# A conditioned transformer block on one core: in the QKV stages, token loads on GpSimd's queue, statistics three products sooner, one set of roots 17 products later

## The chip, the core and the metric

The kernel runs on one core of one Trainium2 chip. The metric is the time of one execution on the device in microseconds (us); of several runs the median is given. The core has a matrix engine (TensorE, in the views PE, with its weight loads as PEld), three more compute engines (VectorE, DVE; ScalarE, ACT; GpSimd, POOL), and SyncE (SP), which here only issues transfers. Each engine takes its instructions in order; transfers can be issued on the queue of SP or on that of GpSimd.

## The reference, cut to what matters

```python
mod = silu(condition) @ Wada + bada
sh_a, sc_a, gt_a, sh_m, sc_m, gt_m = split(mod, 6, axis=1)
xn = layernorm(x, g1, be1)
xm = xn * (1.0 + sc_a[:, None, :]) + sh_a[:, None, :]
x = x + gt_a[:, None, :] * attention(xm, Wqkv, Wproj, bproj)   # causal, 16 heads of 32
xn = layernorm(x, g2, be2)
xm = xn * (1.0 + sc_m[:, None, :]) + sh_m[:, None, :]
h = gelu(xm @ W1 + b1)
x = x + gt_m[:, None, :] * (h @ W2 + b2)
```

`x` has two rows of 2048 tokens with 512 features in float32, `condition` two rows of 512, and the MLP is 2048 wide inside.

## The kernel before, in words

**Stages.** The work runs in this order: QKV of row 0, attention of row 0, projection of row 0 (with the start of row 1's QKV mixed in), QKV of row 1, attention of row 1, projection of row 1, and the MLP over both rows. A row is 16 token tiles of 128 tokens, or four groups of 512 tokens (`NG`, `MTT` = 4 tiles to a group).

**A QKV group.** A group is six units: four of keys and queries, two of values. A unit is seven products of half size (`unit`, L1002), a scheme of Strassen's kind: seven products of sums of blocks in place of eight, into three PSUM banks a, b and c. `first` (L1059) copies a finished bank away on ScalarE, `last` (L1072, L1078) adds a later bank to that copy on VectorE, and `split` (L1064, L1066) makes a high and a low part, which are stored to HBM by SP (L1031). The seventh product of a unit is issued after the first two of the next unit (`run`, L1138). A unit has seven products, so a group has 42 (`STEPS`). The first unit of row 0 alone is done plainly, by eight products of 512 tokens (`plain`).

**What hangs on the products.** After each product `tick` (L1145) runs, with n counting the group's products, and issues what belongs there:

- n = 30: the tokens of the group after the next are loaded (`load_x`, L915), four transfers of 128 tokens on SP's queue. The four buffers named `x` are shared by all groups, so the loads wait until the group before has been transposed out of them.
- n = 10 to 13: the statistics of the next group, one tile each (`stats`, L951 and L216: `bn_stats`, then `bn_aggr` on VectorE); with the fourth, `inv_std` (L223) takes the root of the four variances on ScalarE, then reciprocal and shift on VectorE. For row 1, group 1 has its statistics made during the projection.
- n = 15 and 25: ScalarE scales the next group's first and last two tiles in place (`scaled`, L958, L964).
- n = 18 and 28: TensorE transposes them (`norm`, L970; `transpose`, L214), and the modulated tokens become operands (`xmT`).
- n = 36, 38, 40: sums of operand blocks for the next group (`token_sum`).
- then the stage's own `also`, and from the second group on the first scores of the attention (`score`), with their maxima on VectorE (L498, L504).

**Weight pieces.** `also` calls `pieces.tick` (L1277). `Pieces` (L1207) builds, beside the QKV stages, the sums of MLP weights that the MLP needs: a piece is loaded by SP (L1241), summed by GpSimd (`add`, L1246; L1253) and stored by GpSimd's queue (`store`, L1264; L1273). A tick takes one operation from the list, and two while more than 12 are left. Row 1's plan (L1580) loads and starts four pieces: room_2 at ticks 0 and 6, room_1 at 16 and 24, room_2 again at 47 and 56, room_3 at 74 and 80, ticks counted over all groups. In room_1 a piece is 17 operations: four additions, three times four more, and the store. Row 1's value weights (`load_wv`, L922 on; L936) also come by GpSimd's queue, and their sums (L949) are GpSimd's.

**Order.** Each engine's order is laid down when the program is built. A helper, `mm` for products and `act` for other instructions (L204, L208), pins an instruction behind what its engine was given just before. An instruction without it is placed by a scheduler, which may set it ahead of its place in the program when it holds it for ready. Products, the additions of pieces and the statistics made during projection are pinned; the loads of tokens and the statistics in `tick` are not.

**Projection.** `project_phase` (L1297) computes 16 tiles of one row, takes the statistics for the second norm into `mv2`, and calls `between` after each tile, which for row 0 starts row 1's first group. At its end `inv_std(mv2, ...)` (L1358) takes the roots of the row's 16 variances. The MLP is what uses them.

Of the kernel before, what the change touches and what calls it, by code (L numbers as in the profile page):

```python
# [27 lines left out]
def dit_block_kernel(  # L28
# [36 lines left out]
    nc = tc.nc  # L65
# [4 lines left out]
    NT = T // P  # L70
# [3 lines left out]
    MTT = MT // P  # L74
# [74 lines left out]
    mv2 = const.tile([P, B * NT, 2], F32, tag="mv2", name="mv2")  # L149
    rstd2 = const.tile([P, B * NT], F32, tag="rstd2", name="rstd2")  # L150
    shift1 = const.tile([P, B * NT], F32, tag="shift1", name="shift1")
    shift2 = const.tile([P, B * NT], F32, tag="shift2", name="shift2")
# [47 lines left out]
    def x_rows(n):  # L200
        t0 = (n % NT) * P
        return x[n // NT, t0 : t0 + P, :]
# [5 lines left out]
    def act(ins):  # L208

        return tc.keep_in_program_order(ins)  # L210
# [12 lines left out]
    def inv_std(mv, rstd, shift, lo, hi):  # L223
        nc.scalar.activation(rstd[:, lo:hi], mv[:, lo:hi, 1], AF.Sqrt, bias=eps)
        nc.vector.reciprocal(rstd[:, lo:hi], rstd[:, lo:hi])
        nc.vector.scalar_tensor_tensor(
            shift[:, lo:hi], mv[:, lo:hi, 0], -1.0, rstd[:, lo:hi], ALU.mult, ALU.mult
        )
# [669 lines left out]
    class Qkv:  # L898
# [13 lines left out]
                for n in (S1, S2, A22)  # L912
            }

        def load_x(self, g):  # L915
            xts = []
            for t in range(MTT):
                xt = self.qp.tile([P, D], F32, tag="x", name="x", bufs=4)
                nc.sync.dma_start(xt, x_rows(self.row.b * NT + g * MTT + t))
                xts.append(xt)  # L920
            self.xts[g] = xts

# [190 lines left out]
        def values(self, g, t):  # L1113
# [22 lines left out]
            return self.unit(product, first, last, first)  # L1136

        def run(self, hp, also, early=()):  # L1138

            row = self.row  # L1140
            late = []
            for g in range(NG):
                at = [0]

                def tick():  # L1145
                    n, at[0] = at[0], at[0] + 1
                    if n >= self.STEPS:
                        return
                    if n == 30 and g + 2 < NG:
                        self.load_x(g + 2)  # L1150
                    if g + 1 < NG:
                        if n == 3 and g + 1 not in self.xts:
                            self.load_x(g + 1)
                        if 10 <= n < 10 + MTT and g + 1 > row.b:
                            self.stats(g + 1, n - 10)
                        if n in (15, 25):
                            self.scaled(g + 1, n // 25)
                        if n in (18, 28):
                            self.norm(g + 1, n // 28)()
                        sums = {36: S1, 38: S2, 40: S3}  # L1160
                        if n in sums:
                            self.token_sum(g + 1, sums[n])
                    elif n == 28:

                        row.rows(0)
                        act(nc.scalar.activation(first, eps, AF.Exp))
                    if g > 0 and n == 2:
                        self.token_sum(g, A22)
                    if n > 9 and self.loads:
                        self.loads.pop(0)()  # L1170
                    also(g, n)
                    if g > 0 and n >= 7:


                        past, of = n - 6, self.STEPS - 7
                        if g == 1:
                            row.score(row.count(cum[0] * past / of, 0))
                        else:
                            past += of * (g - 2)
                            row.score(  # L1180
                                row.count(
                                    cum[0] + (cum[2] - cum[0]) * past / (2 * of),
                                    1 if g == 2 and n < 25 else 2,
                                )
                            )

                for u in range(C + 2):
                    if (g, u) in early:
                        for k, step in enumerate(self.plain(g, u, hp)):
                            step()  # L1190
                            if k:
                                tick()
                        self.token_sum(g, S3)
                        continue
                    if u < C:
                        steps = self.keys_and_queries(g, u, hp)
                    else:
                        steps = self.values(g, u - C)
                    for step in steps[:2] + late + steps[2:6]:
                        step()  # L1200
                        tick()
                    late = steps[6:]
            for step in late:
                step()
            assert not self.loads
# [91 lines left out]
    def project_phase(row, psum, between):  # L1297

        b = row.b
        with pool(f"proj{b}") as pp:
            n = 0
            ats = list(row.at_s)
            rbs = {1: row.rb_s[1], 2: row.old_queries(), 3: row.rb_s[0]}
            rows_x = [b * NT + i * TQ + t for i in last_order for t in range(TQ)]
            xts = list(row.xt_s)

            def tokens(upto):  # L1310
                while len(xts) < min(upto, NT):
                    xt = pp.tile([P, D], F32, tag="xt", name="xt", bufs=6)
                    nc.sync.dma_start(xt, x_rows(rows_x[len(xts)]))
                    xts.append(xt)

            row.load_sums(len(units) - 1, len(units))
            tokens(TQ + 6)
            for k, i in enumerate(last_order):
                if k in (0, 1):

                    at = pp.tile([P, C, QB], F32, tag="at", name="at", bufs=2)
                    nc.sync.dma_start(at, od[b][last_order[k + 2]])
                    ats.append(at)
                at = ats[k]
                for t in range(TQ):

                    if n == 0:
                        nc.sync.dma_start(rbs[2], wide_d[b][last_order[2]])
                        nc.sync.dma_start(
                            rbs[3][:, : C - 1], wide_d[b][last_order[3]][:, : C - 1]  # L1330
                        )
                    elif n == 3:
                        row.invert(len(units) - 1, len(units))
                    elif n == 4:
                        row.widen(len(units) - 1, rbs[3][:, C - 1, :])

                    tokens(n + 6)
                    nt, xt = rows_x[n], xts[n]
                    if k > 0:
                        act(nc.gpsimd.tensor_tensor(xt, xt, bgate, ALU.add))  # L1340
                    ps = psum.tile([P, D], F32, tag="mm", name="ps_o")
                    for c in range(C):
                        mm(
                            ps, at[:, c, t * P : (t + 1) * P], row.wproj[:, c, :],
                            start=(c == 0), stop=(c == C - 1),
                        )
                    nc.vector.tensor_tensor(xt, ps, xt, ALU.add)
                    stats(pp, xt, nt, mv2, True)
                    nc.sync.dma_start(x1d[nt], xt)
                    if k + 1 < NQ:  # L1350
                        d = ats[k + 1][:, t, :]
                        act(
                            nc.gpsimd.tensor_tensor(d, d, rbs[k + 1][:, t, :], ALU.mult)
                        )
                    between(n)
                    n += 1
        lo, hi = b * NT, (b + 1) * NT
        inv_std(mv2, rstd2, shift2, lo, hi)  # L1358


    row = Row(0)
    with pool("wada") as wp, pool("qkv0") as qp, pool("hl0") as hp, pool(
# [113 lines left out]
        def also(g, n):  # L1476

            if (g, n) == (0, 7):
                for k in range(4):
                    qkv.weight_sum(nc.gpsimd, k, slice(0, P))  # L1480
            pieces.tick()
            if g == 0 and n == 22:
                load_wada(2, 5)
            elif g in (1, 2) and n == 10:
                qkv.columns = modulation(g + 1)
            elif g in (1, 2) and n == 14:
                qkv.columns()
                if g == 1:
                    load_wada(3, 4)
                else:  # L1490
                    scale_shift(a2, c2, r_g2, r_be2, 3, 4)
# [36 lines left out]
    past, row = row, Row(1)  # L1528
    with pool("qkv1") as qp, pool("ps_qkv1", bufs=6, space=PSUM) as ps_mm:
# [24 lines left out]
        def also(g, n):  # L1554
            if (g, n) == (0, 10):
                qkv.value_weight_sums()
            pieces.tick()

        with pool("hl1") as hp:
# [769 lines left out]
```

## Time and profile before

| quantity | value |
|---|---|
| median of 3 runs | 2249.56 us (2248.82 to 2253.02) |
| the profiled execution | 2252.46 us |
| its span in the trace | 2250.7 us |
| granted TensorE clock, mean | 0.999 |
| instructions | 33467 |
| VectorE busy | 1537.3 us, 68% |
| ScalarE busy | 1003.6 us, 45% |
| GpSimd busy | 1298.3 us, 58% |

The span runs from the first to the last instruction of the one execution that was profiled. A row of a timeline has start and length in us from the span's start, the engine, the line of the kernel, the operation, its tiles (out<-in) with partitions and elements, the count (`x4` is four in a row), and in brackets the idle time of the engine ahead of it with what ended that. `SPq` and `POOLq` are the queues' own work of issuing. Busy times are of the whole span; a share of 68% says nothing of which wait sets the end in one stage.

### The profile page before, as it was taken

How to read it: one execution, taken by the hardware profiler on the slowest of the kernel's cores; microseconds unless marked ns; L12 is line 12 of the kernel's file. 1: busy time of each engine (PE TensorE's matmuls, PEld its weight loads, DVE VectorE, ACT ScalarE, POOL GpSimd, SP SyncE). 2: the span in 40 equal slices, each digit the busy share in tenths (PEclk: the TensorE clock that was granted, in tenths of full speed). 3: DMA queues.
4: the chain of work that ended last, by engine and by line, in shares of the span. 5: the costliest groups of instructions: out<-in, count | busy, mean ns of one | idle time of the engine just before them, and what ended most of it. 6: DMA issues, size and time to landing. Idle time of an engine off the chain costs nothing.

```text
span 2250.7 us, 33467 instructions
## 1 busy us (share of the span) xinstructions
PE 2210.1 (98%) x12057; PEld 1429.4 (64%) x12057; DVE 1537.3 (68%) x3309; ACT 1003.6 (45%) x2012; POOL 1298.3 (58%) x807
## 2 busy tenths in 40 slices
PE   7999999999999999999999999999999999999998
PEld 5887555555543588855555555345787787688687
DVE  4678766777757667777677767663685585576576
ACT  4434555555564253365665556614322422331410
POOL 4253998998983696299989898444105204304210
PEclk9999999999999999999999999999999999999999
DMA  8787142231324799532324113363353354353433
GB/s 274 247 277 193 44 92 70 62 85 48 107 96 135 247 308 321 152 83 67 80 67 104 48 46 131 108 233 127 114 174 131 125 182 147 106 187 126 159 126 109
DMA packets 160510, 311.57 MB, mean 138 GB/s; under 512 B 16544, under 2 KB 48844, under 8 KB 158552
## 3 DMA queue, kind: packets, MB, share of 16 engines
q1 hardware_dynamic: 155488, 285.53, 41.8%
q0 software_dynamic: 4480, 23.36, 2.7%
q8 instruction: 95, 1.56, 0.3%
q14 instruction: 71, 0.58, 0.1%
q10 hardware_dynamic: 376, 0.55, 0.1%
HBM read 229.95 MB, written 87.29 MB: 141 GB/s over the span
## 4 chain that ended last, share of the span: by engine, by line
PE 88%; DVE 4%; POOL 3%; DMA 2%; ACT 1%; issue 1%; SPq 0%; DVEq 0%; ACTq 0%; POOLq 0%
PE ps_a L206 26%; PE st L206 18%; PE ps_b L206 12%; PE o L206 10%; PE s L206 9%; PE ps_c L206 4%; PE sm L206 3%; PE ps_o L206 3%; DVE junk L498 1%; POOL ee L695 1%; PE ps_xt L214 1%; ACT e L670 1%; DVE mx L504 1%; PE ps_o L214 1%; DVE stat L218 1%
## 5 line engine op out<-in xcount | busy, mean ns | idle before, releaser
L670 ACT ACTIVATE e<-st 128x512 f32<-128x512 f32 (+1 forms) x1152 | 575.1, 579 | 362.6 <-PE st L206 319.2
L504 DVE TENSOR_REDUCE mx<-s 128x1 f32<-128x512 f32 x576 | 381.6, 686 | 193.4 <-PE s L206 192.4
L695 POOL TENSOR_TENSOR ee<-ee,e 128x2048 f32<-128x2048 f32 x106 | 485.8, 4583 | 10.4 <-ACT e L670 4.4
L206 PE MATMUL st<-qst,kst 128*128 128x512 f32 (+3 forms) x1280 | 408.8, 386 | 0.0
L206 PE MATMUL s<-kst,qst 128*128 128x512 f32 (+3 forms) x1046 | 380.5, 395 | 6.1 <-DVE mx L504 3.7
L206 PE MATMUL ps_a<-sum,w 128*128 128x256 f32 (+1 forms) x1088 | 328.7, 431 | 0.1
L206 PE MATMUL o<-e,vv 128*32 128x512 f32 (+3 forms) x2560 | 293.2, 537 | 0.3 <-POOL e L682 0.3
L206 PEld LDWEIGHTS st<-qst,kst 128*128 128x128 f32 x1280 | 228.5, 188 | 97.7 <-issue 66.0
L498 DVE CUSTOM_DVE_ANT_0 junk<-s,causal 128x128 bf16<-128x128 f32 (+3 forms) x470 | 220.7, 470 | 61.0 <-PE s L206 47.0
L1797 POOL TENSOR_TENSOR sum<-w 128x256 f32<-128x256 f32 x30 | 22.1, 738 | 395.2 <-PE ps_a L206 263.8
L206 PEld LDWEIGHTS s<-kst,qst 128*128 128x128 f32 x1046 | 194.9, 188 | 71.1 <-DVE mx L504 17.0
L206 PEld LDWEIGHTS ps_a<-sum,w 128*128 128x128 f32 x1088 | 204.5, 190 | 40.1 <-issue 11.4
L695 POOL TENSOR_TENSOR ee<-e 128x2048 f32<-128x2048 f32 x42 | 192.5, 4583 | 43.2 <-ACT e L670 42.3
L206 PEld LDWEIGHTS <-sel 32*128 32x128 bf16 x1152 | 29.5, 91 | 197.0 <-issue 196.1
L2016 ACT ACTIVATE h<-h,cols 128x512 f32<-128x512 f32 x120 | 76.8, 711 | 136.0 <-DVE h L1718 136.0
L504 DVE TENSOR_REDUCE mx<-st 128x1 f32<-128x512 f32 x192 | 131.0, 683 | 0.6
L682 POOL TENSOR_SCALAR_AFFINE_SELECT e<-e 128x512 f32<-128x512 f32 x128 | 83.3, 669 | 67.6 <-ACT e L670 67.5
L206 PE MATMUL st<-fold,sel 32*128 32x512 bf16 (+1 forms) x1152 | 117.5, 372 | 1.3
L206 PEld LDWEIGHTS o<-e,vv 128*32 128x32 f32 x2560 | 59.1, 108 | 92.4 <-issue 73.0
L1718 DVE TENSOR_TENSOR h<-c,ps_b 128x256 f32<-128x256 f32 x90 | 37.9, 421 | 103.5 <-PE ps_b L206 103.0
L1066 POOL TENSOR_TENSOR lo<-lo,hi 128x512 fp32r<-128x512 f32 x32 | 40.6, 1274 | 103.9 <-ACT hi L1064 102.0
L206 PE MATMUL ps_b<-sum,w 128*128 128x256 f32 (+1 forms) x384 | 95.0, 383 | 0.0
(237 smaller groups left out, 3590.2 us busy)
## 6 DMA issues: line engine op xcount, KB each, us to landing
qst<-q SPq DMA_DIRECT2D x128, 256.0 KB
kst<-k SPq DMA_DIRECT2D x128, 256.0 KB
w<-w1d SPq DMA_DIRECT2D x32, 896.0 KB
w<-w2d SPq DMA_DIRECT2D x28, 1024.0 KB
w<-w2d SPq DMA_DIRECT2D x28, 768.0 KB
q<-hi SPq DMA_DIRECT2D x32, 256.0 KB
q<-lo SPq DMA_DIRECT2D x32, 256.0 KB
k<-hi SPq DMA_DIRECT2D x32, 256.0 KB
```

The lines of the kernel that those rows point to most:

```text
L206: return tc.keep_in_program_order(nc.tensor.matmul(*args, **kw))
L214: return tc.keep_in_program_order(nc.tensor.transpose(dst, src, ident[:n, :n]))
L218: ins = nc.vector.bn_stats(st, xt)
L498: nc.vector.tensor_tensor_reduce(junk[:, :w], x, causal[:, QB - w :], 1.0, MASKED, ALU.add, ALU.max, m,)
L504: self.vector(nc.vector.tensor_reduce(m, x, axis=AX.X, op=ALU.max))
L670: act(nc.scalar.activation(e4[:, h, :w], sts[h][:, :w], AF.Exp))
L682: nc.gpsimd.affine_select(d, d, pattern=[[0, HC], [1, P]], compare_op=ALU.is_ge, fill=0.0, base=0, channel_multiplier=-1,)
L695: act(nc.gpsimd.tensor_tensor(dst, x, y, ALU.add))
L1066: engine.tensor_tensor(lo, d, hi.bitcast(F32), ALU.subtract)
L1718: act(nc.vector.tensor_tensor(dst, x, y, ALU.add))
L1797: act(engine.tensor_tensor(dst, u, v, op))
L2016: nc.scalar.activation(d[j], d[j], AF.Gelu, bias=col(r_b1 + half * HF + fs[j], 1))
```

## The change

Three things are edited. The loads at n = 30 are issued on GpSimd's queue instead of SP's, in both rows. The statistics begin at n = 7 instead of 10 in all groups but the first, and the first scaling moves from 15 to 12 with them; where the row's number equals the group's (row 0's first group, row 1's second), the statistics are pinned. And the roots of row 0's projection variances are taken at n = 16 of row 1's first group, not at the end of row 0's projection; row 1's stay where they were.

```diff
-        def load_x(self, g):
+        def load_x(self, g, queue=nc.sync):
             xts = []
             for t in range(MTT):
                 xt = self.qp.tile([P, D], F32, tag="x", name="x", bufs=4)
-                nc.sync.dma_start(xt, x_rows(self.row.b * NT + g * MTT + t))
+                queue.dma_start(xt, x_rows(self.row.b * NT + g * MTT + t))
                 xts.append(xt)
             self.xts[g] = xts
...
                     if n == 30 and g + 2 < NG:
-                        self.load_x(g + 2)
+                        self.load_x(g + 2, nc.gpsimd)
                     if g + 1 < NG:
                         if n == 3 and g + 1 not in self.xts:
                             self.load_x(g + 1)
-                        if 10 <= n < 10 + MTT and g + 1 > row.b:
-                            self.stats(g + 1, n - 10)
-                        if n in (15, 25):
+                        s0 = 7 if g else 10
+                        if s0 <= n < s0 + MTT and g + 1 > row.b:
+                            self.stats(g + 1, n - s0, row.b == g)
+                        if n in (s0 + 5, 25):
                             self.scaled(g + 1, n // 25)
...
                     between(n)
                     n += 1
-        lo, hi = b * NT, (b + 1) * NT
-        inv_std(mv2, rstd2, shift2, lo, hi)
+        if b:
+            inv_std(mv2, rstd2, shift2, NT, 2 * NT)
...
         def also(g, n):
             if (g, n) == (0, 10):
                 qkv.value_weight_sums()
+            elif (g, n) == (0, 16):
+                inv_std(mv2, rstd2, shift2, 0, NT)
             pieces.tick()
```

## The prediction

> **What bounds the kernel now.** I read the page's first part to see which engine has slack, then PE's timeline through the two QKV stages, where the edits lie, then the queues that feed them.
>
> ```profile
> span 2250.7 us, 33467 instructions
> PE 2210.1 (98%) x12057; PEld 1429.4 (64%) x12057; DVE 1537.3 (68%) x3309; ACT 1003.6 (45%) x2012; POOL 1298.3 (58%) x807
> ```
>
> TensorE is busy in 98% of the span: an edit that issues no fewer products can win only the idle time that it closes, 40.6 us in all, and only the part that lies in the QKV stages. PE's timeline of row 0's QKV stage has these stops (time, duration, line, tiles, and in brackets the idle time ahead and who ended it):
>
> ```profile
> 18.28 8.83 PE L206 MATMUL ps_qk<-xmT,wqk 128*128 128x512 f32 x16 [1.78 <-DVE xmT L269]
> ...
> 80.42 0.33 PE L214 MATMUL ps_xt<-ident,x 128*128 128x128 f32 x1 [1.01 <-ACT x L964]
> 81.13 0.98 PE L214 MATMUL ps_xt<-ident,x 128*128 128x128 f32 x7 [0.38 <-ACT x L964]
> ...
> 117.26 1.92 PE L206 MATMUL ps_mod<-vv,sc 128*32 128x512 f32 x16 [0.95 <-DVE mx L504]
> ```
>
> The transposes at 80.42 wait for tokens scaled by ScalarE (1.01 + 0.38 = 1.39). The 0.95 ahead of 117.26 is put down to a maximum on VectorE, which itself stood behind a statistic; its row comes below. Row 1's stage:
>
> ```profile
> 772.07 1.03 PE L206 MATMUL ps_b<-t,wqk 128*128 128x256 f32 x4
> 775.46 1.13 PE L206 MATMUL ps_a<-t,wqk 128*128 128x256 f32 x4 [2.36 <-ACT lo L1059]
> ...
> 825.55 1.89 PE L206 MATMUL ps_a<-t,wqk 128*128 128x256 f32 x8
> ...
> 829.15 0.33 PE L214 MATMUL ps_xt<-ident,x 128*128 128x128 f32 x1 [0.56 <-ACT x L964]
> 829.86 0.98 PE L214 MATMUL ps_xt<-ident,x 128*128 128x128 f32 x7 [0.38 <-ACT x L964]
> ...
> 868.61 0.50 PE L206 MATMUL s<-kst,qst 128*128 128x512 f32 x1 [0.72 <-DVE mx L504]
> ```
>
> Stops of 2.36, 0.94 and 0.72. All that the change can win is therefore 2.36 + 1.39 + 0.95 + 0.94 + 0.72 = 6.36 us, 0.28% of the span.
>
> **The change part by part.**
>
> *The projection's roots.* The longest stop has its cause on ScalarE:
>
> ```profile
> 774.83 0.31 ACT L224 ACTIVATE rstd<-mv,eps 128x16 f32<-128x16 f32 x1 [7.74 <-DVE mv L221]
> ```
>
> The root of row 0's 16 variances waited for the last projection statistic, and the copies of PE's first products (L1059), by which PE's banks come free, stood behind it. The move issues the same three instructions (root, reciprocal, shift) 17 products later, at 16 of row 1's first group, where the variances have long been there; ScalarE is then busy 31.54 of 67.00 us (window below), so 0.31 goes beside PE. Who needs the roots is the MLP, over a thousand us later. Gain 2.36 at most, 0 if the root, which nothing pins, is set back to where it was.
>
> *Row 0's loads.* These are SP's issues of the tokens of groups 2 and 3:
>
> ```profile
> 61.36 1.82 SPq L919 DMA_DIRECT2D x<-in_x_dram  x4
> ...
> 109.96 4.42 SPq L919 DMA_DIRECT2D x<-in_x_dram  x4
> ```
>
> They stood behind stores of keys and queries. The window view shows POOL free here and full in row 1 (length; busy us of PE, PEld, DVE, ACT and POOL with counts; clock, DMA share, GB/s):
>
> ```profile
> 783.00:850.00 67.00, 66.06 (x326) 58.05 (x324) 42.40 (x87) 31.54 (x73) 66.28 (x82) 1.00 0.96 309
> 62.60:100.00 37.40, 36.01 (x184) 29.86 (x183) 20.72 (x62) 17.19 (x39) 0.59 (x1) 1.00 0.85 252
> 850.00:861.00 11.00, 11.00 (x53) 9.61 (x53) 6.79 (x21) 3.81 (x9) 0.20 (x2) 1.00 0.89 355
> ```
>
> POOL does 0.59 us in 37.40, so row 0's loads leave as soon as the old tokens are transposed, and I let the stops of 1.39 and 0.95 go: −2.3. Against that: group 1's statistics, due at 10, are now pinned there. Before, the first ran at
>
> ```profile
> 22.78 0.68 DVE L218 BATCH_NORM_STATS2 stat<-x 128x6 f32<-128x512 f32 x1
> ```
>
> while PE was still in the 16 plain products of 18.28, that is, well ahead of its place in the program. Pinned, the four come later; I take +0.3, one ScalarE root in the way (0.31), between 0 and 1.39 (the stop of 80.42, as the nearest of its kind). Row 0: **−2.0**, and from −2.3 up to +3.1 where a statistic that nothing pins runs ahead of its tokens by the three products it gained (3 × 1.03, row 772.07).
>
> *Row 1, group 2.* Its tokens now leave from SP, and their statistics run here:
>
> ```profile
> 816.59 1.83 SPq L919 DMA_DIRECT2D x<-in_x_dram  x4
> ...
> 860.62 1.82 SPq L919 DMA_DIRECT2D x<-in_x_dram  x4
> ```
>
> ```profile
> 819.49 0.69 DVE L218 BATCH_NORM_STATS2 stat<-x 128x6 f32<-128x512 f32 x1
> ...
> 824.20 0.40 DVE L1078 TENSOR_TENSOR lo<-lo,ps_a 128x256 f32<-128x256 f32 x1
> ```
>
> From SP's issue to the first statistic pass 2.90 us. On POOL the loads take their turn behind additions of MLP weight pieces. The plan starts room_1's 17 operations at tick 24; two a tick at 24, 25 and 26, one at 27, 28 and 29: nine additions come ahead of tick 30, and the tenth is pinned behind the loads. In POOL's timeline:
>
> ```profile
> 780.21 2.90 POOL L936 DMA_DIRECT2D wv<-in_L_cond_Wqkv_dram  x4 [7.09 <-DMA kst<-in_L_cond_W_dram]
> ...
> 812.60 10.79 POOL L1253 TENSOR_TENSOR vv<-vv 128x512 f32<-128x512 f32 x9
> 823.34 0.56 POOL L1273 DMA_DIRECT2D w2d<-vv  x1
> ```
>
> Two of room_1's additions lie just ahead of the nine at 812.60; these take 10.79 / 9 = 1.20 each, so the ninth of the room ends at 812.60 + 7 × 1.20 = 821.0. Four issues take 2.90 (row 780.21); the last begins at about 821.0 + 3 × 0.73 = 823.2. That POOL is busy 66.28 of 67.00 says that it gives no earlier turn unless the loads are set between additions. Landing, for the same 256 KB and for larger stores, takes (last number, us):
>
> ```profile
> wv<-in_L_cond_Wqkv_dram POOLq DMA_DIRECT2D x4, 256.0 KB, 7.6
> ```
>
> ```profile
> w2d<-vv POOLq DMA_DIRECT2D x4, 448.0 KB, 3.6
> ```
>
> The first is of this stage and size, the second of 883 to 893 us. I take 7.6, the nearest: the last token tile is there at about 830.8, between 826.8 and 830.8; as the queue is in use, not all four need the whole 7.6, and I put it at 830. The statistics are now pinned, three products sooner: VectorE stands at them from about 816 until the tokens come, and with it everything behind: maxima of the scores, the joins of L1072 and L1078, by which PE gets banks. The last statistic (0.69) and some six short operations of 0.40 (row 824.20) follow, 3.1 us, an estimate; PE, whose product of 825.55 needs them, goes on at 833.1 to 833.5: +7.6 to +8.0. The stop of 0.94 at 829 falls into it: **+7.0**, between +3.4 (landing 3.6) and +7.0. It takes in the 2.36 won on the roots, as the tokens come at POOL's time and not at PE's.
>
> [...]
>
> [...] The lines view of 783 to 850 has this for GpSimd's issues:
>
> ```profile
> L1273 POOL DMA_DIRECT2D w2d<-vv x6 | 3.3, 548 | 0.0
> ```
>
> [...]
>
> *Row 1, group 3.* The loads go behind room_2's last additions instead of SP's 860.62, from about 851 on (POOL does 0.20 us between 850 and 861; with the first loads it gets there up to 2.9 later). They may end the 0.72, or cost: three products (3.1) plus the slower landing (7.6 − 2.90 = 4.7), +7.8, if these unpinned statistics are set ahead of their tokens. The nearest row for a statistic that waits for tokens:
>
> ```profile
> 115.92 0.69 DVE L218 BATCH_NORM_STATS2 stat<-x 128x6 f32<-128x512 f32 x1 [1.57 <-DMA x<-in_x_dram]
> ```
>
> I take **+1.5**. SP is freed of four issues of 0.46 in each of four groups, 7.3 us of a queue whose waiting is not on PE's path: 0.
>
> *Sum.* −2.0 + 7.0 + 1.5 = +6.5: 2252.46 + 6.5 = 2258.96 for the profiled execution, and on the median, 2249.56 (2.90 lower), **2256.0**.
>
> **The rivals.**
>
> *A, faster: the loads are early.* If the scheduler sets row 1's loads between the additions as soon as the old tokens are transposed, they land before 820 and every stop goes: −6.4, **2243.2**. For it: only additions and products are pinned, not loads. Against it: an addition that is ready and first in the program goes first, and POOL always has one. It decides if the last load starts before some 815: 815 + 7.6 + 3.1 is 825.7, when PE gets there now. If then the root also stays where it was, the change does not do what it says there, −4.0 and 2245.6, still inside A.
>
> *B, no change: the loads are late but quick.* With 3.6 for landing the tokens are there at 826.8, PE goes on at 829.9, +3.4; the third group wins its 0.72: −2.0 + 3.4 − 0.7 = +0.7, **2250.3**. For it the row of 883 to 893, against it the row of the same size, 7.6, at a DMA share of 0.96. [...]
>
> *C, slower still.* The third group's statistics run ahead of their tokens: −2.0 + 7.0 + 7.8 = +12.8, **2262.4**. For it: nothing pins them, and 22.78 shows such ones well ahead of their place. Against it: POOL is free from 850 on.
>
> **How the numbers follow.** Forecast 0.36 (its own range 2253.6, with −2.3 + 7.0 − 0.7, to 2261.2, with row 0 at +3.1), A 0.20, B 0.27, C 0.17. A measurement of this kernel can tell about 0.2%, 4.5 us, from no change, so faster lies under 2245.1 and slower over 2254.1. A gives 0.19 faster and 0.01 same; B 0.27 same; the forecast 0.35 slower and 0.01 same; C 0.17 slower: 0.19, 0.29, 0.52. The range runs from 2244.0 (it leaves out half of A, 0.10) to 2264.0 (half of C, where row 0 is at +3.1 too, 0.08).
>
> **What would show it.** Roots: no root of 16 columns near 774, no stop of 2.36, and one such root some 15 us later. Row 0: issues of tokens on POOL right behind the transposes, and no stop at 80 or ahead of 117. Group 2 of row 1: four issues on POOL between 821 and 824 behind nine additions of room_1, a statistic whose releaser is the DMA of x near 830, and behind it a PE stop of 5 to 8 us released by VectorE. If the issues come before 815, A holds; if the landing is near 3.6, B. If the DMA's landing is 7.6 and PE still does not stop, the chain through the pinned statistics is wrong.

## The result, and the profile after

Over five runs each the changed kernel took a median of 2280.58 us (2274.27 to 2286.7) against 2250.58 (2248.82 to 2253.33): a ratio of 1.0134 with a 95% interval of 1.0113 to 1.0156, slower by 30 us. The forecast had the sign and a fifth of the size. The profiled execution of the changed kernel took 2286.7 us, the longest of its five, so sums made in its trace come to 34 us, not 30.

TensorE's work is the same (12057 products), so the time must be in its stops and its clock (granted 0.993 in the mean, 0.999 before). The first lines of the page after:

```profile
span 2285.0 us, 33456 instructions
## 1 busy us (share of the span) xinstructions
PE 2221.7 (97%) x12057; PEld 1435.7 (63%) x12057; DVE 1539.9 (67%) x3309; ACT 1003.6 (44%) x2012; POOL 1303.2 (57%) x823
```

PE is busy 11.6 us longer with the same products, and the span has grown by 34.3. Where that happens is read off a fixed point of each group, the start of its transposes (L214) in PE's timelines of both kernels (groups are numbered from 0, as in the code; some expectations below call row 1's group 2 its second group):

| transposes | before | after | after − before |
|---|---|---|---|
| row 0, group 1, first | 38.92 | 41.34 | +2.42 |
| row 0, group 1, second | 48.43 | 53.18 | +4.75 |
| row 0, group 2, first | 80.42 | 88.27 | +7.85 |
| row 0, group 3, first | 129.35 | 140.05 | +10.70 |
| row 1, group 0 (within the projection), second | 746.30 | 758.06 | +11.76 |
| row 1, group 1, first | 790.24 | 800.31 | +10.07 |
| row 1, group 2, second | 839.83 | 854.87 | +15.04 |
| row 1, group 3, first | 873.58 | 903.94 | +30.36 |
| projection of row 1 (transposes there) | 1480.10 | 1513.67 | +33.57 |

What lies between these stages, and the MLP, adds about 1 us and less each. Row 0 loses 8.3 us between the first and the fourth line, row 1 gains 1.7 where the roots stood, then loses 5.0 in group 2, 15.3 in group 3 and 3.2 behind it; 2.4 lie ahead of all this (last section). The stops of PE that carry these steps, in PE's timeline after:

```profile
41.34 0.33 PE L214 MATMUL ps_xt<-ident,x 128*128 128x128 f32 x1 [1.58 <-ACT x L964]
42.04 1.41 PE L214 MATMUL ps_xt<-ident,x 128*128 128x128 f32 x7 [0.38 <-ACT x L964]
...
62.66 3.55 PE L206 MATMUL ps_a<-wv,t 128*128 128x256 f32 x8 [2.40 <-DVE vv L1134]
```

```profile
785.52 1.13 PE L206 MATMUL ps_a<-t,wqk 128*128 128x256 f32 x4 [0.67 <-ACT lo L1059]
...
831.52 2.00 PE L206 MATMUL ps_a<-t,wqk 128*128 128x256 f32 x8 [1.43 <-DVE lo L1078]
839.91 2.00 PE L206 MATMUL ps_a<-t,wqk 128*128 128x256 f32 x8 [1.60 <-DVE lo L1078]
...
869.98 2.07 PE L206 MATMUL ps_b<-wv,t 128*128 128x256 f32 x4 [13.84 <-DVE lo L1072]
...
926.33 0.61 PE L206 MATMUL s<-kst,qst 128*128 128x512 f32 x1 [3.17 <-DMA qst<-q]
```

The stop of 2.36 is down to 0.67. In its place stands one of 13.84, put down to a join of VectorE (L1072). VectorE's own timeline shows what the join stood behind:

```profile
851.08 0.08 DVE L498 DVE_READ_ACCUMULATOR2_ANT mx<- 128x1 f32 x1
866.70 0.69 DVE L218 BATCH_NORM_STATS2 stat<-x 128x6 f32<-128x512 f32 x1 [15.54 <-DMA x<-in_x_dram]
...
869.51 0.42 DVE L1072 SCALAR_TENSOR_TENSOR lo<-ps_b,lo 128x256 f32<-128x256 f32 x1
```

For 15.54 us VectorE did nothing but wait for the tokens of row 1's last group, with the join that PE needed behind two of the statistics and their maxima. Row 0 shows the same on a smaller scale:

```profile
48.98 0.69 DVE L218 BATCH_NORM_STATS2 stat<-x 128x6 f32<-128x512 f32 x1 [3.36 <-DMA x<-in_x_dram]
...
60.32 0.69 DVE L218 BATCH_NORM_STATS2 stat<-x 128x6 f32<-128x512 f32 x1 [8.07 <-DMA x<-in_x_dram]
```

There the loads themselves leave sooner than before: GpSimd issues those of group 2 at 43.82 and 54.65, two each, right behind the transposes, where SP's stood at 61.36.

A group's statistics are due at n = 7 of the group ahead of it, yet these stand at a place of VectorE's order that PE reaches in the middle of the group before that one. How far ahead is counted in the instruction order of the built programs: the joins of VectorE (L1072, L1078 and L1134, three to a unit) ahead of the four statistics of a group, counted from the start of row 0:

| statistics of | before | changed | e2, queue alone | e4, all pinned |
|---|---|---|---|---|
| row 0, group 2 | 19 to 21 | 6 to 12 | 6 to 12 | 18 |
| row 0, group 3 | 36 | 24 to 27 | 24 to 27 | 36 |
| row 1, group 2 | 90 to 93 | 90 | 81 to 84 | 90 |
| row 1, group 3 | 109 to 111 | 96 to 101 | 96 to 101 | 108 |

Nine to thirteen joins are three to four units, 21 to 30 products, not the three products that the diff names. The one group of these that the change pins (row 1, group 2) is not ahead.

### The profile page after: what moved, and what is told of

It is laid out like the page before. It is cut to its first block, busy times and chain, and to the rows that moved or that the text cites. A ratio compares the mean times of both kernels' runs of the same rounds, so it can differ in the third digit from the quotient of the medians.

```text
span 2285.0 us, 33456 instructions
## 1 busy us (share of the span) xinstructions
PE 2221.7 (97%) x12057; PEld 1435.7 (63%) x12057; DVE 1539.9 (67%) x3309; ACT 1003.6 (44%) x2012; POOL 1303.2 (57%) x823
## 4 chain that ended last, share of the span: by engine, by line
PE 85%; DVE 4%; POOL 4%; DMA 3%; issue 2%; ACT 1%; SPq 1%; DVEq 0%; POOLq 0%; ACTq 0%
PE ps_a L206 24%; PE st L206 18%; PE ps_b L206 11%; PE o L206 10%; PE s L206 9%; PE ps_o L206 4%; PE sm L206 3%; PE ps_c L206 3%; POOL ee L695 1%; DVE junk L498 1%; PE ps_xt L214 1%; ACT e L670 1%; DMA x<-in_x_dram 1%; DVE mx L504 1%; PE ps_o L214 1%
## 5 line engine op out<-in xcount | busy, mean ns | idle before, releaser
L1066 POOL TENSOR_TENSOR lo<-lo,hi 128x512 fp32r<-128x512 f32 x32 | 40.6, 1272 | 125.7 <-ACT hi L1064 122.5
```

The source lines that it names most:

```text
L1066: engine.tensor_tensor(lo, d, hi.bitcast(F32), ALU.subtract)
```

## The experiments

**Theory P (placement).** With the loads on GpSimd's queue the scheduler holds the tokens for ready soon after their buffers are free, and sets the unpinned statistics there; VectorE then waits for loads that are late, and what follows in its order waits behind them (15.54 us above). **Rival W**: the loads themselves are too late on GpSimd's queue, wherever the statistics stand. **Rival S**: taking the statistics three products sooner is the cost.

**e1, the roots alone.**

```diff
-        inv_std(mv2, rstd2, shift2, lo, hi)
+        if b:
+            inv_std(mv2, rstd2, shift2, NT, 2 * NT)
...
+            elif (g, n) == (0, 16):
+                inv_std(mv2, rstd2, shift2, 0, NT)
```

> Only the roots of row 0's projection variances move; the loads stay on SP, the statistics at 10. Theory P (placement: with the loads on GpSimd's queue the unpinned statistics are set some 12 joins, four units, ahead of their place and hold VectorE until the tokens land): 1 to 2.4 us faster than before, the stop of 2.36 gone, all else as before. Rival W (the loads themselves come too late on GpSimd's queue): the same. Rival S (the statistics three products sooner are what costs): the same. It prices the move alone.

Measured: 2251.72 against 2252.06, ratio 0.9999 (0.9991 to 1.0008). The stop is down from 2.36 to 0.67 as with the change, but the root has not moved: in e1 it stands at 771.40, still directly ahead of the copies of L1059. What P expected, 1 to 2.4 us, is not seen (0.3 by the medians), and what the move is worth this run cannot tell. No theory is hurt; the edit is not what costs.

**e2, the queue alone.**

```diff
-                        self.load_x(g + 2)
+                        self.load_x(g + 2, nc.gpsimd)
```

> Only the queue of the loads changes; statistics at 10 and unpinned, roots as before. P: all three groups' statistics of row 1 and row 0 that have such loads are set ahead (row 1's group 2 too, which the change had pinned), so at least as slow as the change: 25 to 45 us over before. W: 15 to 30 us over before. S: within 5 us of before.

Measured: 2292.75, ratio 1.0186 (1.0172 to 1.02), 41 us slower, and 11 more than the whole change, each against its own runs of before. That lies in P's range and above W's; S falls, as nothing is sooner here. VectorE waits in row 1's group 2 too, which the change had pinned:

```profile
825.33 0.69 DVE L218 BATCH_NORM_STATS2 stat<-x 128x6 f32<-128x512 f32 x1 [18.48 <-DMA x<-in_x_dram]
...
874.74 0.69 DVE L218 BATCH_NORM_STATS2 stat<-x 128x6 f32<-128x512 f32 x1 [10.82 <-DMA x<-in_x_dram]
```

**e3, the statistics sooner alone** (with the scaling at 12 and the two pins, loads on SP).

```diff
-                        if 10 <= n < 10 + MTT and g + 1 > row.b:
-                            self.stats(g + 1, n - 10)
-                        if n in (15, 25):
+                        s0 = 7 if g else 10
+                        if s0 <= n < s0 + MTT and g + 1 > row.b:
+                            self.stats(g + 1, n - s0, row.b == g)
+                        if n in (s0 + 5, 25):
```

> Only the statistics move to 7 (with the first scaling at 12 and the two pins); loads on SP, roots as before. P and W: within 4 us of before, stops of the kind of 1 us only. S: 20 us or more over before.

Measured: 2253.92 against 2252.06, ratio 1.0012 (1.0004 to 1.0021). That is 1 to 5 us slower, within the 4 us of P and W by the medians (1.9), and far from S's 20: S is out.

**e4, the change with every statistic pinned.**

```diff
-                            self.stats(g + 1, n - s0, row.b == g)
+                            self.stats(g + 1, n - s0, True)
```

> The change, with every statistic pinned at its place, loads on GpSimd's queue. P: the long waits of VectorE for tokens go in row 0 and in row 1's group 3; row 1's group 2 keeps its 4 to 7 us; 2246 to 2258 in all. W: the tokens are late for statistics at their place as well, 2268 or more. S: as slow as the change, 2280.

Measured: 2260.97, ratio 1.004 (1.0027 to 1.0053). One argument and no other instruction: of the 30 us over before 8.9 are left, 21 are gone, and the placement in the table above with them. VectorE's waits for tokens in the QKV stages, up to 15.54 us in the change, are 0.84 at most. That is P, and W, which had 2268 or more, is out as an account of the whole. But 2261 lies over P's range, and the trace tells of two places. At row 1's group 2 PE waits 2.42, 1.96 and 1.37, and at row 1's first scores 5.02:

```profile
817.57 1.99 PE L206 MATMUL ps_a<-t,wqk 128*128 128x256 f32 x8 [2.42 <-DVE lo L1078]
826.32 3.19 PE L206 MATMUL ps_a<-t,wqk 128*128 128x256 f32 x8 [1.96 <-DVE lo L1078]
844.78 1.13 PE L206 MATMUL ps_a<-t,wqk 128*128 128x256 f32 x4 [1.37 <-DVE lo L1078]
...
900.52 0.77 PE L206 MATMUL s<-kst,qst 128*128 128x512 f32 x1 [5.02 <-DMA qst<-q]
```

In row 0, on the other hand, the transposes of group 3 start at 126.08, 3.27 ahead of before, against 0.62 ahead at group 1's: the stops of 1.39 and 0.95 are closed, as the prediction had it, once the statistics stand at their place.

**e5, as e4 with row 1's loads on SP.**

```diff
-                        self.load_x(g + 2, nc.gpsimd)
+                        self.load_x(g + 2, nc.sync if row.b else nc.gpsimd)
```

> As e4 (every statistic pinned at its place, roots moved), but row 1's loads go back to SP; only row 0's are on GpSimd's queue. Theory P (placement): row 0 keeps the 2.7 us that e4 showed there, the roots their 1.7, and row 1 loses nothing: 2245 to 2250, the fastest so far. Rival W (loads on GpSimd's queue come too late everywhere): 2253 or more. If the 7 us that e4 lost at row 1's first scores come from SP's order and not from row 1's loads, they stay: 2254 or more.

Measured: 2250.63 against 2251.89, ratio 0.9996 (0.9987 to 1.0005). This is 0.6 over P's range, and no faster than before by more than the interval; it is against W, which had 2253 or more. Row 1's remaining loss is from row 1's loads.

**e6, as e4 with all statistics at 10.**

```diff
-                        s0 = 7 if g else 10
+                        s0 = 10
```

> As e4, but all statistics at 10 and pinned there, the first scaling at 15. If row 1's second group lost its 5.9 us in e4 because its tokens miss a place three products early, about 3 us of that come back and the stops of 2.42 and 1.96 shrink to under 1 each: 2256 to 2259. If the place does not matter, 2261 as e4.

Measured: 2264.69, ratio 1.0059 (1.0046 to 1.0072). A miss, and of the wrong sign: later statistics are slower than sooner ones. The wait only moves: in row 1's group 2 PE stops 0.37 ahead of the join and 3.81 at the transposes, whose tokens cannot be scaled without the statistics. Row 0's stops of 1.03 and 0.38 are back as well, so the early loads alone do not close them. Nor does the sooner scaling gain without the early loads: e3 has no stop at these transposes, but others of 0.50 to 1.93 us in row 0.

**e7, as e4 with room_1's additions behind the loads.**

```diff
-                (room_2, 0, 6), (room_1, 16, 24), (room_2, 47, 56), (room_3, 74, 80),
+                (room_2, 0, 6), (room_1, 16, 31), (room_2, 47, 56), (room_3, 74, 80),
```

> As e4, but room_1's additions start at tick 31, behind the loads, not at 24. If it is GpSimd's turn that makes row 1's second group late, its four issues leave before 815 instead of about 815 to 822 in e4, the stops of 2.42 and 1.96 go, and 4 to 6 us come back: 2255 to 2257. If it is the landing (5 us and more), the stops stay and the time is 2261.

Measured: 2255.79, ratio 1.0018 (1.0009 to 1.0027), 5 us under e4. GpSimd's timeline of e4 has its four issues apart, between additions and stores:

```profile
809.58 0.56 POOL L919 DMA_DIRECT2D x<-in_x_dram  x1
810.17 3.31 POOL L1254 TENSOR_TENSOR vv<-vv 128x512 f32<-128x512 f32 x4
813.43 0.56 POOL L919 DMA_DIRECT2D x<-in_x_dram  x1
814.01 1.95 POOL L1254 TENSOR_TENSOR vv<-vv 128x256 f32<-128x256 f32 x2
815.90 1.11 POOL L1274 DMA_DIRECT2D w2d<-vv  x2
817.00 1.08 POOL L919 DMA_DIRECT2D x<-in_x_dram  x2
```

and that of e7 has them in a row, ten us earlier for the last:

```profile
806.13 2.13 POOL L919 DMA_DIRECT2D x<-in_x_dram  x4
```

So the loads' place among room_1's operations is what cost in row 1's group 2 of e4: from group 1's second transposes to group 2's PE takes 45.58 us in e4, 41.31 in e7 and 40.08 before. The stop of 2.42 is down to 0.26, that of 1.96 only to 1.63.

That late tokens are the way to this cost is not shown, though. In e4 VectorE waits for these tokens only 0.84 and 0.45 us, and the stop of 2.42 comes ahead of the first statistic. It stands behind two instructions of VectorE (L997, a block sum, and L1066, a low part) that took 4.32 and 2.56 us from 809.72 on; in e7, where the stop is 2.16 shorter, they took an estimated 4.7 together (4.32 + 2.56 − 2.16). In row 0's stretch with a free GpSimd (62.60 to 100.00, before) both take 0.69. In e4 GpSimd was busy with additions and issues for 6.76 of those 6.80 us. No run parts the two.

**e8, the loads on SP and the statistics ahead by hand.**

```diff
-                        if 10 <= n < 10 + MTT and g + 1 > row.b:
+                        if 10 <= n < 10 + MTT and g == 0 and row.b == 0:
                             self.stats(g + 1, n - 10)
+                        if 31 <= n < 31 + MTT and g + 2 < NG:
+                            self.stats(g + 2, n - 31, True)
...
-                nc.vector.tensor_tensor(d, d, ps, ALU.add)
+                act(nc.vector.tensor_tensor(d, d, ps, ALU.add))
```

The joins of L1072, L1078 and L1134 are all pinned in this way, since otherwise they are set ahead of the statistics again.

> The kernel before, loads on SP, nothing on GpSimd's queue, roots as before; but the statistics of groups 2 and 3 are taken right behind the loads of their tokens, at 31 to 34 of the group before the last, and they and the joins of VectorE are pinned, so that they stand about where the change's unpinned ones stood (8 to 9 joins ahead of their place). P: VectorE waits for tokens and PE behind it as under the change, 20 to 45 us over before, with no load on GpSimd's queue. W: within 5 us of before, since the loads are SP's.

Measured: 2305.39, ratio 1.0235 (1.0221 to 1.0249), 53 us slower and more than P expected. The run does not decide between P and W: in its trace the pinned joins make waits of their own. PE's stops behind VectorE in the QKV stages come to some 43 us, while VectorE waits for tokens 4.7 us in all (3.11 of them just ahead of PE's longest stop of 9.10). No run pins the joins alone.

**e9, as e4 with row 1's last group on SP.**

```diff
-                        self.load_x(g + 2, nc.gpsimd)
+                        self.load_x(g + 2, nc.sync if row.b and g else nc.gpsimd)
```

> As e4, but the tokens of row 1's last group are loaded by SP again; row 1's third group and row 0 stay on GpSimd's queue. If the stop of 5.02 at row 1's first scores (they wait for a load of queries that stands one store later on SP's queue than before) comes from taking these four issues off SP's queue, it goes: 2252 to 2256. If it comes from the third group's delay, it stays: 2259 to 2262.

Here the third group is the one that this document calls group 2, and the last is group 3. Measured: 2263.86, ratio 1.0051 (1.0038 to 1.0063), above both ranges. The stop at the first scores stays, at 5.46: those four issues are not its cause.

**e10, e7 and e9 together.**

> As e7 (pinned statistics, roots moved, room_1's additions behind the loads), with the tokens of row 1's last group on SP as in e9. Where the theory holds in all its parts, nothing that the change costs is left, and its gains stay: 2244 to 2249, faster than both kernels. Where the wait at the first scores has another cause: 2255.

Measured: 2256.7, ratio 1.0026 (1.0017 to 1.0035). A miss. Up to group 3 of row 1 it runs 5.7 us ahead of before (the second transposes start at 880.12, not 885.86), and then loses all of it and more at one stop at the first scores:

```profile
893.19 0.76 PE L206 MATMUL s<-kst,qst 128*128 128x512 f32 x1 [5.58 <-DMA qst<-q]
```

SP's timeline of e10 shows which queue they wait in:

```profile
868.52 0.38 SPq L1031 DMA_DIRECT2D k<-hi  x1
884.87 0.34 SPq L1031 DMA_DIRECT2D k<-lo  x1
885.25 2.54 SPq L360 DMA_DIRECT2D qst<-q  x2
```

and that of the kernel before:

```profile
875.44 0.38 SPq L1031 DMA_DIRECT2D k<-hi  x1
880.23 0.34 SPq L1031 DMA_DIRECT2D k<-lo  x1
880.62 0.92 SPq L360 DMA_DIRECT2D qst<-q  x2
```

Both have the loads of queries behind the store of a low part, and that store waits for GpSimd's split (L1066). Before, the split stands behind seven additions of room_3, at 878.93; in e9 and e10 it stands behind the whole piece (892.05 and 883.56). GpSimd in e10:

```profile
880.85 1.10 POOL L1274 DMA_DIRECT2D w2d<-vv  x2
881.94 1.07 POOL L1274 DMA_DIRECT2D w2d<-kst  x2
883.00 0.54 POOL L1274 DMA_DIRECT2D w2d<-qst  x1
883.56 4.95 POOL L1066 TENSOR_TENSOR lo<-lo,hi 128x512 fp32r<-128x512 f32 x4
```

**e11, the change with row 1's statistics pinned, row 0's left as they are.**

```diff
-                            self.stats(g + 1, n - s0, row.b == g)
+                            self.stats(g + 1, n - s0, row.b == g or row.b == 1)
```

> The change, with row 1's statistics pinned and row 0's left unpinned as the change has them. It parts the loss by rows: row 0's unpinned statistics stand 9 to 12 joins early and should keep their loss of some 11 us against e4, row 1's last group should lose its 15: 2268 to 2273. If row 0's loss is not from the placement, 2261 as e4.

Measured: 2272.23, ratio 1.0089 (1.0074 to 1.0104): 11 us over e4 and 10 under the change, each against its own runs of before. By rows, the placement costs some 11 us in row 0 and 10 in row 1. In the profiled executions row 1's share is larger: the first transposes of its group 3 are 11.75 late in e11 and 30.36 in the change.

**e12, as e10 with room_3's additions from tick 96.**

```diff
-                (room_2, 0, 6), (room_1, 16, 31), (room_2, 47, 56), (room_3, 74, 80),
+                (room_2, 0, 6), (room_1, 16, 31), (room_2, 47, 56), (room_3, 74, 96),
```

> As e10, but the additions of row 1's last piece (room_3) start at tick 96, not at 80, so that on GpSimd's queue a split of a low part stands behind 6 of them as in the kernel before (7 there), and not behind the whole piece as in e9 and e10. If the stop of 5.58 at row 1's first scores comes from that split (a store of keys waits for it on SP's queue, and the loads of queries behind the store), it shrinks under 1 and the time falls by 5 to 8 us: 2246 to 2251, at or under the kernel before. If it comes from elsewhere, 2256 as e10.

Measured: 2248.9 against 2250.99, ratio 0.9989 (0.998 to 0.9998). The split stands behind six additions again and no stop at the first scores is longer than 0.30:

```profile
873.46 2.52 POOL L1254 TENSOR_TENSOR vv<-vv 128x512 f32<-128x512 f32 x2
875.93 1.28 POOL L1066 TENSOR_TENSOR lo<-lo,hi 128x512 fp32r<-128x512 f32 x1
```

It is 6.7 us under e10, each against its own runs of before, and by 2.5 us (0.4 to 4.5) the one version of the twelve whose interval clears the kernel before, if barely. So that split is what the stop at the first scores came from in e10.

## Why the prediction was wrong

- **What bounds the kernel, and the most that can be won**: right in the main. Nothing won more than the 6.36 us of stops; e12 won 2.5. The list of row 0's stops left out one of 1.26 us ahead of 109.07, behind a copy of L1059; it is there in e1, e4 and e12 too (1.26 or 1.27), so the change does not touch it.
- **The roots**: the case that the prediction priced at 0 is the one that came. In the change the root of 16 columns still stands behind the last projection statistic and ahead of PE's first copies:

```profile
784.89 0.31 ACT L224 ACTIVATE rstd<-mv,eps 128x16 f32<-128x16 f32 x1 [6.65 <-DVE mv L221]
785.11 0.36 ACT L1059 ACTIVATE lo<-ps_a 128x256 f32<-128x256 f32 x1
```

  It is so in every version that has the edit. The stop went from 2.36 to 0.67 because the last projection statistic comes sooner behind PE's last projection product (that root starts 1.77 us behind the product's end, 3.46 before); but it is 1.40 in e3 without the edit, and 1.22 and 2.26 in e7 and e12 with it. Why it differs is open, and the 1.7 us in the trace is not the move's.
- **Row 0, taken as −2.0 with an upper end of +3.1**: the step that failed first. The gain of 2.3 is there in e4 (2.7), but in the change the statistics of groups 2 and 3 stand far ahead of their tokens, and the row loses 8.3 between its first and last transposes in the table (2.3 of them at group 1, next point). I had quoted the row that shows unpinned statistics running ahead (22.78) and then priced such a step at the three products by which the diff moves it. By P, how far it can go is set by when the scheduler holds its input for ready, and the new queue changed that: e2, which moves no statistic in the program, has the same places.
- **Group 1's pinned statistics, +0.3**: too small. Their root is done at 39.85 instead of 29.36, PE stops 1.58 + 0.38 us at the transposes of 41.34, and the products behind run at a lower clock (0.61 from 42.04 to 46.44; 1.00 before from 41 to 46). From the first product behind the plain unit to group 1's second transposes the change takes 23.95 us against 21.48, +2.5, and e4 22.29, +0.8. Every version that has this pin has the stop (1.58 to 2.06), and none of the four without it (before, e1, e2, e8).
- **Row 1's group 2, +7.0**: the size came out near (5.0 in the change, 5.5 in e4), by luck in good part. The forecast had VectorE stand at the statistics from 816 until the last tokens landed, and one stop of 5 to 8 us behind that. In the change VectorE waits for them only 0.83 us, and PE stops three times (1.43, 1.60 and 1.70), the first ahead of any statistic. VectorE was then at two instructions that took more than twice as long as before. In the change and in the kernel before:

```profile
824.67 3.31 DVE L997 TENSOR_TENSOR t<-xmT,t 128x512 f32<-128x512 f32 x1 [1.22 <-PE ps_a L206]
827.90 2.58 DVE L1066 TENSOR_TENSOR lo<-lo,hi 128x512 fp32r<-128x512 f32 x1
```

```profile
813.77 0.69 DVE L997 TENSOR_TENSOR t<-xmT,t 128x512 f32<-128x512 f32 x1 [2.17 <-PE ps_a L206]
814.38 1.76 DVE L1066 TENSOR_TENSOR lo<-lo,hi 128x512 fp32r<-128x512 f32 x1
```

  Together that is 5.89 us against 2.45. GpSimd was busy nearly all that time in both (5.79 of 5.81 us and 2.29 of 2.37), and in the change the loads stand among its additions; but e7, where none stands there, has an estimated 4.7 (experiment e7), while in e10 with the same plan PE has no stop there (815.06). Why VectorE takes longer is open. The working was off in both halves: three additions of room_1 stand ahead of the first load (823.53) and not nine, so that the four issues are spread over 8 us among the additions and stores, where I had them in one block, and the landing is shorter than the 7.6 that I took:

```profile
x<-in_x_dram POOLq DMA_DIRECT2D x8, 256.0 KB, 4.8
```

  This is the median over groups 2 and 3 of row 1 (2.9 to 8.7), between the 3.6 and the 7.6 of the prediction's two rows.
- **Row 1's group 3, +1.5 with an upper end of +7.8**: the term that was most wrong, 15.3. It was rival C's mechanism, to which I gave 0.17, at twice its price. The argument against C was that GpSimd is free from 850 on; after the change it is not:

```profile
848.66 1.26 POOL L1254 TENSOR_TENSOR kst<-kst,qst 128x512 f32<-128x512 f32 x1 [7.77 <-DMA qst<-in_L_cond_W_dram]
```

  The same addition, the first of room_2's second piece, stood 18 us earlier in the kernel before:

```profile
830.54 1.28 POOL L1253 TENSOR_TENSOR kst<-kst,qst 128x512 f32<-128x512 f32 x1
```

  GpSimd waited 7.77 us for the piece's weights, and the tokens' loads, among that piece's operations, left from 862.38 on. So a delay on one queue became one on the next; what made the weights late was not tried.
- **SP's relief, 0**: wrong in kind. What counts is not SP's time but the order that the schedule gives to SP and GpSimd. e10 and e12 show that one split behind a whole piece is worth 6.7 us at row 1's first scores. The same chain stands in e4, where PE stops 5.02 for these loads: GpSimd's split behind the whole piece, then SP's store of the low part, then the loads.

```profile
890.59 4.96 POOL L1066 TENSOR_TENSOR lo<-lo,hi 128x512 fp32r<-128x512 f32 x4
```

```profile
891.90 0.34 SPq L1031 DMA_DIRECT2D k<-lo  x1
892.29 2.54 SPq L360 DMA_DIRECT2D qst<-q  x2
```

  The change has it at 916.56, 917.87 and 918.26, ahead of its stop of 3.17. In these two no run moved room_3.

The step that failed, in one sentence: the prediction let statistics that nothing pins move by the three products of the diff, and priced group 3 of row 1 at +1.5 on a GpSimd that was free; they moved by nine to thirteen joins and held VectorE for up to 15.54 us at once, and pinning them gave back 21 of the 30 us.

What stays open: why the scheduler sets statistics so early when their tokens come by GpSimd's queue. The orders show that it does, and pinning shows what it costs; its reasons were not tried.

## What to carry to other kernels

When a transfer is moved to another queue, look at who consumes it, not only at when it leaves: here the consumers that nothing pinned moved with the new queue, and on their engine they then held up work that has nothing to do with them, for up to 15.54 us. Compare the order of the consumers' engine in both programs, and pin the consumers first: here one argument was worth 21 us. And look for a moved instruction in the engine's own order: the roots were moved in the program and nowhere else. The gain of a few us in these stages was kept only once the next queue's order was looked at as well (e10 against e12).

## What the runs showed of the hardware

Behind some stops of PE the granted clock was lower, so that such a stop cost more than its length. The four products of 869.98, behind the stop of 13.84, took 2.07 us against 1.03 elsewhere, and the clock was 0.50 from 869.98 to 872.90. In the windows view of the changed kernel the stretch around this stop has this (length; busy PE, PEld, DVE, ACT, POOL; clock; DMA share; GB/s):

```profile
840.00:870.00 30.00, 14.46 (x75) 12.32 (x75) 8.02 (x24) 10.62 (x24) 22.01 (x33) 0.80 0.95 311
870.00:900.00 30.00, 30.00 (x127) 25.70 (x128) 19.73 (x53) 11.47 (x26) 5.70 (x6) 0.91 0.59 197
```

The eight products behind the stop of 2.40 in row 0 took 3.55 us against 1.89 elsewhere, at a clock of 0.54. It does not go by length alone: in e4 eight products behind a stop of 2.42 took 1.99 us, and eight behind one of 1.96 took 3.19. What decides it, no run shows. The clock differs at the kernel's start too: its first 16 plain products took 8.83 us in the profiled execution of before, 10.18 in that of the change and 7.13 in e4's, at clocks of 0.91, 0.82 and 1.00 from 17 to 36 us. In the change the products behind them start 2.28 us later than before, 1.35 of it from these 16, which themselves start 0.93 later. Two stops of before (0.89 and 0.22) are missing in the change, which leaves 0.68 us of that ahead of group 1's transposes; the stop of 1.58 there brings the first line of the table to +2.42. Between these profiled executions the same 16 products thus differ by up to 3 us (7.13 to 10.18).

VectorE's sums of two operands of 128x512 (L997, L1066) took 0.68 or 0.69 us each beside a free GpSimd (0.59 us busy in 37.40, before), and up to 4.32 beside one that was busy throughout (6.76 of 6.80 us, e4). Before has one of 0.69 beside a busy GpSimd as well (813.77; GpSimd's additions run from 812.60 to 823.39), so that is not the whole of it; no run here parts its additions from its issues.
